# Layer norm of two graph-attention layers: the statistics of a row from an addition with a sum and a Square with a sum

## The chip, the cores and the metric

The kernel runs on one core of a Trainium2 chip. The metric is the device time of one execution in microseconds (us). The kernel before took 1764.37 us, the median of three runs (1763.55, 1764.37 and 1769.72). One further execution was profiled, at 1764.85 us; all views below come from it.

## The reference

Four graph layers on 3327 nodes with 512 features and one adjacency matrix (3327 x 3327 integers, mostly zero). Each layer adds its result to its input and normalises every row:

```
def _layernorm(x, axis=-1, eps=1e-5):
    m = jnp.mean(x, axis=axis, keepdims=True)
    v = jnp.var(x, axis=axis, keepdims=True)
    return (x - m) / jnp.sqrt(v + eps)

x = _layernorm(x + L0(x, adj, W, a1, a2))      # graph attention, 8 heads of 64
x = _layernorm(x + L1(x, adj, ...))            # mean over neighbours
x = _layernorm(x + L2(x, adj, ...))            # mean over the first 64 neighbours
x = _layernorm(x + L3(x, adj, W, a))           # graph attention, 4 heads of 128
```

In layers 0 and 3, for every head, e_ij = leaky_relu(f1_i + f2_j, 0.2) where there is an edge, attention = softmax(e) over j, and the head's result is elu(attention @ Wh), heads side by side. So the row that is normalised is x + elu(h).

## The kernel before

**Tiling.** The nodes lie in 26 blocks of 128 (the partitions). For every block the kernel makes a list of the edges (`structure`, L863) and later gathers one table row per edge with indirect DMAs, issued by GpSimd (POOL): 128 rows at a time are a chunk, up to four chunks a group (`gather`, L1006). A group (`Gat.group`, L1274) compares positions (`far` on ACT, `ds` on DVE), adds scores (`sc` on DVE, L1337 and L1339), takes their Exp on ACT (L1340, L1341), makes the 0/1 selection matrix `sel` (ACT), multiplies the gathered rows by the weights on DVE (L1348, tile `gt`, `gl` or `gk`), and adds them up per node with matmuls on TensorE (PE) into `acc` in PSUM (L1367). Layer 3 has a dense part for the first block's column: `upc` is made on ACT (four instructions, L1404) and DVE (L1406), and goes into `acc` by L1364. Layer 0 has a dense row (`Gat.dense`, L1449: `gd` on ACT, `raw` on DVE, `acct` on PE).

**The end of a block**, in layers 0 and 3 (`Gat.summed`, L1520): ACT divides the heads (`h`, L1518) and takes Exp of them (`e`, L1528); DVE adds max(h, 0) to the residual (`h`, L1530) and then min(e, 1) to that (`e`, L1531). Now `e` is the row to be normalised (the constant -1 of elu does not change a normalised row). `moments` (L803) makes mean and variance with DVE's statistics pass (`st`, L805) and its aggregation (`mv`, L807). The reciprocal root `rs` comes in layer 0 from POOL (`rstd`, two operations, L815 and L816), in layer 3 from Ln and Exp on ACT and three small steps of refinement on DVE (`power`, L831 and L832, and `newton`, L838 to L840). DVE multiplies -mean by `rs` (`nm`, L859) and ACT writes the normalised row (`scaled_by_act`, L860), to `xres` in layer 0 and to `o`, which SP's queue stores to the output, in layer 3. Layer 0 then transposes the row on PE, copies it on ACT (`xt`, L786), multiplies it with one or two weights (`po`, L800), and stores the result for layer 1 (`t`, `zb`).

**What sets the order.** The work is written as generators that yield between stages, and the stages of several blocks and groups are interleaved. Up to L1781 a scheduler then orders each engine's instructions by its own estimates, so layer 0's order can change with any edit. From L1781 on (layers 1 to 3) the order is as written. `rstd` yields `AHEAD` = 2 times ahead of its POOL operations. In layer 0 each tile of a block's end (`h`, `e`, `mv`, `nm`, `rs`) has one buffer, in layer 3 two. Each engine runs its queue in order, and a waiting instruction holds what is behind it.

Of the kernel before, what the change touches and what calls it, by code (L numbers as in the profile page):

```python
# [8 lines left out]
F32 = mybir.dt.float32  # L9
# [8 lines left out]
AF = mybir.ActivationFunctionType  # L18
ALU = mybir.AluOpType
# [4 lines left out]
P = 128  # L24
BIG = 1e30
EPS = 1e-5
# [515 lines left out]
AHEAD = 2  # L542
# [89 lines left out]
def sparse_path(ctx, tc, flag_i, x, adj, l0_w, l0_a1, l0_a2, l1_w_self, l1_b_self, l1_w_nb, l1_b_nb,  # L632
# [13 lines left out]
    nc = tc.nc  # L646
    N, D = x.shape
# [11 lines left out]
    def pool_in(lay, name, bufs=1, **kw):  # L659
        return lay.enter_context(tc.tile_pool(name=name, bufs=bufs, reuse_waits="tile", **kw))  # L660
# [69 lines left out]
    eps = const.tile([P, 1], F32, name="s_eps")  # L730
    nc.gpsimd.memset(eps, EPS)
    mhalf = const.tile([P, 1], F32, name="s_mhalf")
# [22 lines left out]
    H0, _, OUT0 = l0_w.shape  # L755
    H3, _, OUT3 = l3_w.shape
# [12 lines left out]
    def store(dst_d, b, t, shift=0):  # L769
        for p0, p1 in rows_of(b):  # L770
            nc.sync.dma_start(dst_d[shift + b * P + p0:shift + b * P + p1, :], t[p0:p1])
# [7 lines left out]
    def transposed(pool, ps, src, xsum=None, b=0):  # L779

        pt = ps.tile([P, DC, P], F32, name="pt", tag="tr")
        for c in range(DC):
            nc.tensor.transpose(pt[:, c, :], src[:, c * P:(c + 1) * P], ident)  # L783
        xt = pool.tile([P, DC, P], F32, name="xt")
        if xsum is None:
            nc.scalar.copy(xt, pt)  # L786
            return xt
        n = LAST if b == NB - 1 else P
        for c in range(DC):
            nc.scalar.activation(xt[:, c, :n], pt[:, c, :n], AF.Identity, accum_out=xsum[:, c, b:b + 1])  # L790
        if n < P:
            xs = pool.tile([P, DC], F32, name="xs")
            nc.vector.tensor_reduce(xs, xsum, AX.X, ALU.add)
            nc.vector.tensor_scalar(xt[:, :, n], xs, 1.0 / N, None, ALU.mult)
        return xt

    def times(ps, xt, w):
        po = ps.tile([P, D], F32, name="po")
        for c in range(DC):
            nc.tensor.matmul(po, xt[:, c, :], w[:, c], start=c == 0, stop=c == DC - 1)  # L800
        return po

    def moments(fin, y):  # L803
        st = fin.tile([P, 6], F32, name="st")
        nc.vector.bn_stats(st, y)  # L805
        mv = fin.tile([P, 2], F32, name="mv")
        nc.vector.bn_aggr(mv, st)  # L807
        return mv

    def rstd(fin, mv):  # L810

        for _ in range(AHEAD):
            yield
        rs = fin.tile([P, 1], F32, name="rs")
        nc.gpsimd.tensor_scalar(rs, mv[:, 1:2], EPS, 1.0, ALU.add, ALU.mult)  # L815
        nc.gpsimd.tensor_tensor(rs, rs, mhalf, ALU.pow)  # L816
        yield
        return rs

    def root(fin, mv):  # L820

        r0 = fin.tile([P, 1], F32, name="r0")
        nc.scalar.activation(r0, mv[:, 1:2], AF.Sqrt, bias=eps)
        yield
        nc.vector.reciprocal(r0, r0)
        return newton(fin, mv, r0)
# [27 lines left out]
    def scaled(o, y, mv, rs):  # L854
        nc.vector.tensor_scalar(o, y, mv[:, 0:1], rs, ALU.subtract, ALU.mult)  # L855

    def scaled_by_act(o, y, fin, mv, rs):
        nm = fin.tile([P, 1], F32, name="nm")
        nc.vector.scalar_tensor_tensor(nm, mv[:, 0:1], -1.0, rs, ALU.mult, ALU.mult)  # L859
        nc.scalar.activation(o, y, AF.Identity, bias=nm, scale=rs)  # L860


    def structure(big, mid, ps, m0):  # L863
# [167 lines left out]
    class Gat:  # L1031
# [488 lines left out]
        def summed(self, fin, acc, xb):  # L1520

            hq = acc
            if isinstance(acc, list):
                hq = fin.tile([P, D], F32, name="h")
                self.divided(fin, acc, hq)
                self.held[acc.turn] = 0
            e = fin.tile([P, D], F32, name="e")
            nc.scalar.activation(e, hq, AF.Exp)  # L1528
            yield
            nc.vector.scalar_tensor_tensor(hq, hq, 0.0, xb, ALU.max, ALU.add)  # L1530
            nc.vector.scalar_tensor_tensor(e, e, 1.0, hq, ALU.min, ALU.add)  # L1531
            mv = moments(fin, e)
            rs = yield from (rstd if self.k == 0 else power)(fin, mv)
            return e, mv, rs

    def by_heads(w, c, H):

# [18 lines left out]
    xres = [wpool.tile([P, D], F32, name=f"xres{b}") for b in range(NB)]  # L1556
# [17 lines left out]
    with ExitStack() as pro:  # L1574
# [18 lines left out]
        g0 = Gat("g0", t0_d, H0, OUT0, w0, 0)  # L1593
# [91 lines left out]
    fin = pool_in(lay, "l0f", side="right")  # L1685
# [4 lines left out]
    def layer0(b, acc):  # L1690
        work.add(layer0_end(b, acc))

    def layer0_end(b, acc):
        yield
        x1 = xres[b]
        e, mv, rs = yield from g0.summed(fin, acc, x1)
        scaled_by_act(x1, e, fin, mv, rs)
        xt = transposed(fin, ps, x1)
        yield
        t2 = fin.tile([P, 2, D], F32R, name="t2", bufs=2)  # L1700
        po = times(ps, xt, wn)
        nc.scalar.copy(t2[:, 0], po)
        nc.vector.tensor_sub(t2[:, 1], po, t2[:, 0].bitcast(F32))
        store(t1_d, b, t2.bitcast(F32).rearrange("p s d -> p (s d)"), 2)
        if b >= NB - LATE0:
            return
        if b:
            yield
        zb = fin.tile([P, D], F32, name="zb0", tag="e")
        nc.scalar.copy(zb, times(ps, xt, wx))  # L1710
        store(z1_d, b, zb)
# [140 lines left out]
    def both():  # L1852
        work.step()
        ends.step()
# [9 lines left out]
    with ExitStack() as lay:  # L1864
        fin = pool_in(lay, "l1f", 2)
# [91 lines left out]
        for item in woven(ring):  # L1957
            b, at = item[0], item[4]
# [33 lines left out]
    with ExitStack() as lay:  # L1992
        fin = pool_in(lay, "l2f", 2)
# [6 lines left out]
        g3 = Gat("g3", t3_d, H3, OUT3, w3, 1)  # L2000
# [84 lines left out]
    with ExitStack() as lay:  # L2085
        pools = (Ring(H3 * (OUT3 + 2), extra, rows), pool_in(lay, "l3s", 3),
                 pool_in(lay, "l3pa", 2, space=PSUM), pool_in(lay, "l3p1", 3, space=PSUM))
        fin = pool_in(lay, "l3f", 2)

        def layer3(b, acc):  # L2090
            ends.add(layer3_end(b, acc))

        def layer3_end(b, acc):
            yield
            e, mv, rs = yield from g3.summed(fin, acc, xres[b])
            o = fin.tile([P, D], F32, name="o")
            scaled_by_act(o, e, fin, mv, rs)
            store(out, b, o)

        def verdict():  # L2100

            yield
            bad = fin.tile([P, 4, NL], F32, name="bad")
            nc.vector.memset(bad, 0.0)
            nc.vector.tensor_tensor(bad[:, 0, :], deg[:, 1:], cnt, ALU.not_equal)
            used = fin.tile([P, 3, NL], F32, name="used")
            room = fin.tile([P, 3, NL], F32, name="room")
            nc.vector.tensor_add(used[:, 1:], starts.rearrange("p l s -> p s l"), dgs.rearrange("p l s -> p s l"))
            nc.vector.tensor_add(used[:, 0], used[:, 1], used[:, 2])
            for ls in lists:  # L2110
                for l in ls:
                    for k, n in enumerate((l.room, l.near, l.far)):
                        nc.gpsimd.memset(room[:, k, l.at:l.at + 1], float(n))
            yield
            nc.vector.tensor_tensor(bad[:, 1:], used, room, ALU.is_gt)
            tot = fin.tile([P, 2], F32, name="tot")
            nc.vector.tensor_reduce(tot[:, 0:1], bad, AX.XY, ALU.add)
            nc.vector.tensor_reduce(tot[:, 1:2], spread, AX.X, ALU.add)
            nc.vector.tensor_add(tot[:, 0:1], tot[:, 0:1], tot[:, 1:2])
            yield  # L2120
            pt = pools[3].tile([P, 512], F32, name="pg")
            nc.tensor.matmul(pt[0:1, 0:1], tot[:, 0:1], ones[:, 0:1], start=True, stop=True)
            nc.vector.tensor_copy(flag_i, pt[0:1, 0:1])

        ends.newest = True
        ends.add(g3.open_column(fin))
        for k, item in enumerate(groups(pools[0], range(1, NB), first=(1, 2))):
            if item[4] == 0:
                ends.add(g3.column(item[0], fin))
            work.add(g3.group(item, pools, accs, layer3, sall))  # L2130
            both()
            if k == 6:
                ends.add(layer3_end(0, bias1))
            if k == 12:
                ends.add(verdict())
        while work.live or ends.live:
            both()


@with_exitstack  # L2140
def kernel(ctx: ExitStack, tc: tile.TileContext, *args):


    nc = tc.nc
    pool = ctx.enter_context(tc.tile_pool(name="flagp", bufs=1))
    flag_i = pool.tile([1, 1], I32, name="flag_i")
    sparse_path(tc, flag_i, *args)
    again = nc.values_load(flag_i[0:1, 0:1], min_val=0, max_val=1 << 20)
    with tc.If(again > 0):
        general_path(tc, *args)  # L2150
# [30 lines left out]
```

## Time and profile before

| what | us |
|---|---|
| runs shown, median (range) | 1764.37 (1763.55 to 1769.72) |
| profiled execution | 1764.85 |
| its span, first to last instruction | 1763.1 |
| layer 0: lists and projection, then groups with ends | 0 to 290, 290 to 735 |
| layers 1 and 2 | 735 to 1475 |
| layer 3 | 1475 to 1763 |
| L805 (`st`), 104 in all four layers, 26 in each | 0.695 each (median) |
| L807 (`mv`), 104 | 0.182 each (median) |
| L1531 (`e`), 52 in layers 0 and 3 | 0.692 each (median) |

In the profile, busy time is given for each engine: PE for matmuls, PEld for weight loads, DVE for VectorE, ACT for ScalarE, POOL for GpSimd. The chain of work that ended last is followed back from the last instruction to what released each step; an engine's share in it is time for which this engine was what everything waited for. A timeline row gives start, duration, engine, line, operation, output and input tiles, and in square brackets how long the engine had been idle and what ended that. A stretch is a window of the span with the busy time of each engine in it, the granted TensorE clock, the busy share of the DMA engines and GB/s. A source row gives the smallest, median and largest duration in ns.

### The profile page before, as it was taken

What the parts mean: (1) busy time and instruction counts of PE and PEld (TensorE: products, weight loads), DVE (VectorE), ACT (ScalarE), POOL (GpSimd) and SP (SyncE); (2) the same over time, 40 slices, a digit from 0 to 9 for tenths busy, and PEclk for the clock granted to TensorE, in tenths of its full rate; (3) what the DMA queues carried; (4) which work ended last, traced back from release to release, by engine and by line L of the source; (5) the groups of instructions that cost most, each with busy time, mean ns of one, the idle gap of its engine ahead of it and who ended that gap; (6) DMA issues with size and microseconds to landing.
All of it is one profiled execution on the core that took longest, in us unless ns stands there. A gap on an engine that the chain in (4) does not pass through costs nothing.

```text
span 1763.1 us, 24351 instructions
## 1 busy us (share of the span) xinstructions
PE 1505.3 (85%) x7266; PEld 1002.5 (57%) x7266; DVE 1219.4 (69%) x3292; ACT 872.8 (50%) x2922; POOL 760.5 (43%) x909
## 2 busy tenths in 40 slices
PE   5979847889999989889999999856999973878885
PEld 4756536656666667445555554422666752767664
DVE  8989859988668788225656785537666542867897
ACT  5879645656657767312122121211444442556786
POOL 3000146555454620164444652266656206666640
PEclk9989878999999999889999999988999996979998
DMA  8787667666665542298988995387878416767761
GB/s 258 260 274 240 210 190 247 216 185 200 189 188 154 173 123 80 82 401 292 303 287 306 342 371 191 98 285 247 279 255 269 153 43 189 198 199 211 225 198 56
DMA packets 130401, 381.98 MB, mean 217 GB/s; under 512 B 22037, under 2 KB 36477, under 8 KB 130259
## 3 DMA queue, kind: packets, MB, share of 16 engines
q0 software_dynamic: 67696, 252.97, 45.2%
q1 hardware_dynamic: 62563, 127.35, 21.4%
q8 instruction: 60, 0.98, 0.2%
q14 instruction: 82, 0.67, 0.1%
HBM read 331.89 MB, written 48.37 MB: 216 GB/s over the span
## 4 chain that ended last, share of the span: by engine, by line
PE 57%; DVE 17%; ACT 9%; issue 7%; another core or an unknown queue 4%; DMA 3%; POOL 2%; SPq 0%; DVEq 0%; POOLq 0%; ACTq 0%
PE po L800 18%; PE acc L1367 10%; PE acc L1844 9%; PE po L1048 8%; PE pt L783 3%; DVE cand L912 2%; DVE gt L1348 2%; DVE gl L1348 1%; PE acc L1836 1%; DVE st L805 1%; PE acct L1477 1%; PE acc L1255 1%; ACT h L1518 1%; DVE e L1531 1%
## 5 line engine op out<-in xcount | busy, mean ns | idle before, releaser
L1010 POOL DMA_INDIRECT gt<-t_d,idx x201 | 204.0, 1015 | 369.0 <-DVE mx L1147 197.4
L1010 POOL DMA_INDIRECT gl<-t_d,idx x265 | 261.6, 987 | 185.7 <-issue 56.7
L1367 PE MATMUL acc<-gt,sel 128*128 128x264 f32 (+3 forms) x804 | 208.2, 404 | 3.4 <-issue 1.9
L800 PE MATMUL po<-wn,xt 128*128 128x512 f32 x416 | 197.5, 618 | 15.5 <-ACT xt L786 5.8
L1010 POOL DMA_INDIRECT gm<-t_d,idx x138 | 136.1, 986 | 132.7 <-PE acc L1844 79.1
L1367 PEld LDWEIGHTS acc<-gt,sel 128*128 128x128 f32 (+3 forms) x804 | 150.7, 197 | 41.0 <-issue 15.9
L1367 PE MATMUL acc<-gl,sel 128*128 128x260 f32 (+3 forms) x524 | 140.3, 412 | 14.5 <-issue 11.0
L800 PEld LDWEIGHTS po<-wn,xt 128*128 128x128 f32 x416 | 79.3, 197 | 101.8 <-issue 79.4
L1048 PE MATMUL po<-gt,xt 128*128 128x268 f32 x416 | 115.9, 424 | 15.2 <-ACT xt L790 10.9
L1348 DVE TENSOR_TENSOR gt<-gt,pg 128x1536 f32<-128x1536 f32 (+3 forms) x63 | 116.4, 1848 | 14.8 <-ACT sel L1343 12.5
L1367 PEld LDWEIGHTS acc<-gl,sel 128*128 128x128 f32 (+3 forms) x524 | 100.6, 202 | 34.7 <-issue 15.6
L1844 PE MATMUL acc<-gm,selr 128*128 128x512 f32 (+3 forms) x324 | 106.6, 452 | 5.5 <-DMA gm<-t_d,idx 5.1
L1010 POOL DMA_INDIRECT gk<-t_d,idx x65 | 67.4, 1037 | 95.5 <-DMA t_d<-mean 58.6
L912 DVE MAX8 cand<-val 128x8 f32<-128x464 uint16 (+32 forms) x184 | 107.8, 622 | 0.0
L1048 PE MATMUL po<-w,xt 128*128 128x262 f32 x416 | 98.7, 391 | 9.6 <-ACT xt L790 5.8
L786 ACT COPY xt<-pt 128x512 f32<-128x512 f32 x81 | 46.9, 587 | 119.3 <-PE pt L783 83.6
L1048 PEld LDWEIGHTS po<-gt,xt 128*128 128x128 f32 x416 | 78.6, 202 | 34.7 <-ACT xt L790 14.5
L1300 ACT ACTIVATE far<-place,nmids 128x384 int16<-128x384 int16 (+3 forms) x167 | 88.2, 544 | 13.8 <-DVE ds L1310 9.9
L1048 PEld LDWEIGHTS po<-w,xt 128*128 128x128 f32 x416 | 78.9, 192 | 27.3 <-ACT xt L790 10.0
L800 PE MATMUL po<-wx,xt 128*128 128x512 f32 x208 | 93.5, 594 | 0.0
L800 PE MATMUL po<-wl,xt 128*128 128x512 f32 x208 | 93.0, 592 | 0.0
L783 PE MATMUL pt<-s_ident,xres 128*128 128x128 f32 x500 | 78.8, 285 | 10.4 <-DVE xres L855 5.3
(377 smaller groups left out, 3268.5 us busy)
## 6 DMA issues: line engine op xcount, KB each, us to landing
ab<-in_adj_dram SPq DMA_DIRECT2D x25, 832.0 KB
ab<-in_adj_dram SPq DMA_DIRECT2D x25, 831.5 KB
t_d<-t SPq DMA_DIRECT2D x25, 512.0 KB
gm<-t_d POOLq DMA_DIRECT2D x23, 512.0 KB
t_d<-t SPq DMA_DIRECT2D x25, 384.0 KB
t_d<-tg SPq DMA_DIRECT2D x25, 264.0 KB
gd<-t_d SPq DMA_DIRECT2D x25, 264.0 KB
t_d<-tg SPq DMA_DIRECT2D x25, 260.0 KB
```

What stands on the lines that cost most here:

```text
L783: nc.tensor.transpose(pt[:, c, :], src[:, c * P:(c + 1) * P], ident)
L786: nc.scalar.copy(xt, pt)
L800: nc.tensor.matmul(po, xt[:, c, :], w[:, c], start=c == 0, stop=c == DC - 1)
L805: nc.vector.bn_stats(st, y)
L912: nc.vector.max(out=cand[:, s, :], in_=val[:, cuts[s]:cuts[s + 1]])
L1010: nc.gpsimd.indirect_dma_start(out=t[:m, c, :], out_offset=None, in_=table[:, :], in_offset=bass.IndirectOffsetOnAxis(ap=l.idx[:m, c0 + c: ...
L1048: nc.tensor.matmul(pw[s], xt[:, c, :], self.w[:, c, s, :], start=c == 0, stop=c == DC - 1)
L1255: nc.tensor.matmul(self.acc[h // hh][:, h % hh, :], wt[:m, h, :], G[:m, h, :], start=False, stop=False)
L1300: nc.scalar.activation(o, place[:, (c0 + q0) * P:(c0 + q1) * P], AF.Abs, bias=l.nmid[:, k:k + 1], scale=2.0)
L1348: nc.vector.tensor_mul(Gc[:, :, :OUT], Gc[:, :, :OUT], w[:, :g].rearrange("p c (h o) -> p (c h) o", o=1).to_broadcast([P, g * H, OUT]))
L1367: nc.tensor.matmul(accs[b][s], S[:m, c, :], G[:m, c, s * hh * M:(s + 1) * hh * M], start=at + c == 0, stop=last)
L1844: nc.tensor.matmul(accs[b], chosen, parts[:, k * D:(k + 1) * D], start=at + c + k == 0, stop=k == top and at + c == n - 1)
```

## The change

The row's sum comes out of the addition L1531 (`accum_out`, a sum along the row); DVE turns it into -mean with one multiplication of a 128x1 column. ACT squares the centred row (`e` plus -mean as a bias column) with a sum of its own, which gives 512 times the variance; the squares themselves go into `h`, which is not needed any more. `moments` is not called in these two layers. `rs` is made from the second sum with the same operations as before (POOL in layer 0; Ln, Exp and three steps on DVE in layer 3), the factor 1/512 taken into their constants. The last product is -mean times `rs`. Layers 1 and 2 are as before.

```diff
-    def rstd(fin, mv):
...
-    def scaled_by_act(o, y, fin, mv, rs):
-        nm = fin.tile([P, 1], F32, name="nm")
-        nc.vector.scalar_tensor_tensor(nm, mv[:, 0:1], -1.0, rs, ALU.mult, ALU.mult)
-        nc.scalar.activation(o, y, AF.Identity, bias=nm, scale=rs)
+    def scaled_by_act(o, y, nm, rs):
+        nc.vector.tensor_mul(nm[:, 0:1], nm[:, 0:1], rs)
+        nc.scalar.activation(o, y, AF.Identity, bias=nm[:, 0:1], scale=rs)
...
             nc.vector.scalar_tensor_tensor(hq, hq, 0.0, xb, ALU.max, ALU.add)
-            nc.vector.scalar_tensor_tensor(e, e, 1.0, hq, ALU.min, ALU.add)
-            mv = moments(fin, e)
-            rs = yield from (rstd if self.k == 0 else power)(fin, mv)
-            return e, mv, rs
+            nm = fin.tile([P, 2], F32, name="nm")
+            nc.vector.scalar_tensor_tensor(e, e, 1.0, hq, ALU.min, ALU.add, accum_out=nm[:, 0:1])
+            nc.vector.tensor_scalar(nm[:, 0:1], nm[:, 0:1], -1.0 / D, None, ALU.mult)
+            nc.scalar.activation(hq, e, AF.Square, bias=nm[:, 0:1], accum_out=nm[:, 1:2])
+            if self.k == 0:
+                for _ in range(AHEAD):
+                    yield
+                rs = fin.tile([P, 1], F32, name="rs")
+                nc.gpsimd.tensor_scalar(rs, nm[:, 1:2], 1.0 / D, EPS, ALU.mult, ALU.add)
+                nc.gpsimd.tensor_tensor(rs, rs, mhalf, ALU.pow)
+                yield
+            else:
+                r0 = fin.tile([P, 1], F32, name="r0")
+                nc.scalar.activation(r0, nm[:, 1:2], AF.Ln, bias=eps, scale=1.0 / D)
+                nc.scalar.activation(r0, r0, AF.Exp, scale=-0.5)
+                yield
+                rs = fin.tile([P, 1], F32, name="rs")
+                nc.vector.scalar_tensor_tensor(rs, nm[:, 1:2], EPS * D, r0, ALU.add, ALU.mult)
+                nc.vector.scalar_tensor_tensor(rs, rs, -0.5 / D, r0, ALU.mult, ALU.mult)
+                nc.vector.scalar_tensor_tensor(rs, rs, 1.5, r0, ALU.add, ALU.mult)
+            return e, nm, rs
```

The two callers, `layer0_end` (L1693) and `layer3_end` (L2093), hand `nm` on in place of `mv`.

More of the change, by code (lines that the diff above doesn't have):

```diff
@@ L808, in moments @@
         return mv
-    def rstd(fin, mv):
[L812 to L818, printed above, removed]
     def root(fin, mv):
@@ L1695, in layer0_end @@
         x1 = xres[b]
-        e, mv, rs = yield from g0.summed(fin, acc, x1)
-        scaled_by_act(x1, e, fin, mv, rs)
+        e, nm, rs = yield from g0.summed(fin, acc, x1)
+        scaled_by_act(x1, e, nm, rs)
         xt = transposed(fin, ps, x1)
@@ L2094, in layer3_end @@
             yield
-            e, mv, rs = yield from g3.summed(fin, acc, xres[b])
+            e, nm, rs = yield from g3.summed(fin, acc, xres[b])
             o = fin.tile([P, D], F32, name="o")
-            scaled_by_act(o, e, fin, mv, rs)
+            scaled_by_act(o, e, nm, rs)
             store(out, b, o)
```

## The prediction

> **What bounds the kernel now.** I read the page's busy row and the chain's shares first, then the busy time by stretch, then the timeline of DVE and ACT around the ends of blocks, and last the waits.
>
> ```profile
> PE 1505.3 (85%) x7266; PEld 1002.5 (57%) x7266; DVE 1219.4 (69%) x3292; ACT 872.8 (50%) x2922; POOL 760.5 (43%) x909
> ...
> PE 57%; DVE 17%; ACT 9%; issue 7%; another core or an unknown queue 4%; DMA 3%; POOL 2%; SPq 0%; DVEq 0%; POOLq 0%; ACTq 0%
> ```
>
> Over the whole span PE carries the chain; DVE has 17% of it. The change touches only the ends of blocks in layer 0 (290 to 735 us) and layer 3 (1500 to 1763 us), so the stretches count (us, then busy time of PE, PEld, DVE, ACT, POOL):
>
> ```profile
> 290.00:400.00 110.00, 93.53 (x462) 65.62 (x463) 96.23 (x303) 67.21 (x198) 61.62 (x63) 0.89 0.67 209
> 400.00:500.00 100.00, 94.92 (x438) 63.31 (x437) 71.75 (x204) 62.54 (x200) 50.22 (x61) 1.00 0.63 190
> 600.00:735.00 135.00, 121.02 (x673) 88.32 (x672) 98.57 (x194) 87.82 (x331) 24.09 (x28) 0.96 0.32 99
> 1600.00:1700.00 100.00, 83.18 (x527) 66.62 (x528) 85.74 (x225) 76.28 (x236) 63.01 (x65) 0.95 0.75 219
> ```
>
> Layer 0 is DVE's until 400 (96 of 110), PE's to 600, then shared. In layer 3 from 1600 on DVE and ACT are both nearly full. There the timeline shows a loop. DVE, one block:
>
> ```profile
> 1689.76 0.69 DVE L1530 SCALAR_TENSOR_TENSOR h<-h,xres 128x512 f32<-128x512 f32 x1
> 1690.49 0.69 DVE L1531 SCALAR_TENSOR_TENSOR e<-e,h 128x512 f32<-128x512 f32 x1
> 1691.21 0.69 DVE L805 BATCH_NORM_STATS2 st<-e 128x6 f32<-128x512 f32 x1
> 1691.94 0.18 DVE L807 BATCH_NORM_AGGREGATE mv<-st 128x2 f32<-128x6 f32 x1
> 1692.04 1.19 DVE L1348 TENSOR_TENSOR gl<-gl,pg 128x1024 f32<-128x1024 f32 x1
> ```
>
> and ACT in the same block:
>
> ```profile
> 1689.10 0.63 ACT L1528 ACTIVATE e<-h 128x512 f32<-128x512 f32 x1
> ...
> 1690.84 0.60 ACT L1300 ACTIVATE far<-place,nmids 128x384 int16<-128x384 int16 x1
> 1692.16 0.29 ACT L831 ACTIVATE r<-mv,s_eps 128x1 f32<-128x1 f32 x1 [0.72 <-DVE mv L807]
> ...
> 1696.83 0.63 ACT L1528 ACTIVATE e<-h 128x512 f32<-128x512 f32 x1
> ```
>
> DVE's addition starts 0.03 after the Exp ends (1689.73); four DVE instructions later Ln starts (1692.16) after an idle 0.72; from Ln ACT runs without a gap to the next Exp's end (1697.46), where DVE's next addition starts. The period, 7.73, is 2.43 of DVE and 5.30 of ACT, and DVE is full meanwhile too.
>
> **The change, part by part** (us per block; 26 blocks in each layer).
>
> DVE loses st and mv. In the loop above the product L1348 starts 1.55 after e's start. Afterwards e's addition carries an accumulator read, and one 128x1 multiply follows. Nearest rows:
>
> ```profile
> L926 DVE TENSOR_SCALAR_CACHE_REDUCE some<-sl x25: 160/177/203, 44.1 to 415.2; 128x24 f32<-128x24 f32 x17, 128x32 f32<-128x32 f32 x5, 128x40 f32<-128x40 f32 x2, 128x48 f32<-128x48 f32 x1
> L926 DVE DVE_READ_ACCUMULATOR some<-sl x25: 77/84/90, 44.2 to 415.3; 128x1 f32 x25
> ...
> L790 ACT ACTIVATION_READ_ACCUMULATOR xt<-pt x208: 194/222/323, 17.6 to 1444.9; 128x1 f32 x104
> ```
>
> The read starts some 0.07 before its addition ends and takes 0.08, so the sum stands about 0.70 after e's start. The multiply starts 0.03 later (the gap between L838 and L839) and takes 0.15 (L928); an independent product may start 0.10 after it (mv to L1348 above). That is 0.84 in place of 1.55: **DVE gains 0.71 per block**, if the addition stays at 0.69 with a sum. No row here has a large addition with a sum. From below it is 0.69; from above 1.22: 0.69 holds 512 elements and about 0.16 of fixed cost (the 128x1 rows), so half the rate adds 0.53. I take 0.69, since L926 at 24 to 48 elements is only 0.03 above the 128x1 rows, and keep 1.22 for the range.
>
> [...]
>
> ACT gains a Square of 128x512 with a column as bias. Exp without a column is 0.63 and L860 with two is 0.80 (layer 3): 0.72 between them; then the read, 0.20 (L884: 0.18 to 0.20), starting 0.10 before the Square ends. In ACT's queue that is 0.62 + 0.09 = **0.71 per block**; from below 0.53 (Exp's slot), from above 0.94. Ln and Exp stay, and both programs load three tables.
>
> The path from e to Ln: sum 0.70, multiply to 0.885, 0.04 to cross (mv to Ln), Square and read 0.82, 0.035 to Ln: 1.78 after e's start, in place of 1.67 (1690.49 to 1692.16): **0.12 later**. ACT's idle 0.72 covers the Square: it is free at 1691.44, the multiply is done at about 1691.38. Where that cover is gone, the 0.71 is paid whole. The product nm x rs takes the place of L859 at the same 0.16; layer 0's two POOL operations stay two. The junk output goes into h, which the same engine rewrites later, in order: no new wait for a buffer.
>
> Queued behind the new wait (Square for the multiply) are ACT's upc x4, Exp of the scores, sel and far; DVE waits for upc, PE for sel.
>
> **Layer 3.** For each block I took from the timeline how late DVE starts h after the Exp. Blocks 0 to 7 (to 1620): PE and the gathers decide; L1340 waits 1.3 to 12.1 in seven of the eight, which hides 0.12: nothing. From block 8 on:
> - DVE late by 0.38 to 0.86 (into blocks 9, 12, 13, 20, 21), or ACT itself waiting 1.46 for DVE's sc (into 14): DVE's 0.71 counts until ACT's path, 0.12 later, decides: into 9, 12, 13, 14, 20, 21 that is -0.70, -0.71, -0.30, -0.71, -0.32, -0.60 = -3.34.
> - Exp on time, late by 0.03 or held by upc (into 10, 16 to 19, 25, and the tail after 25): 7 x 0.12 = +0.84.
> - the other five (into 11, 15, 22, 23, 24), with smaller slack either way: +0.10, -0.03, 0, -0.10, 0 = -0.03.
> Sum -2.5.
>
> **Layer 0.** Ends at 302, 333 and 354 lie on the chain while it runs on DVE: 3 x -0.71 = -2.1. From 400 to 600 PE is at 94 of 100 and hides both. From 640 to 690 the chain alternates between DVE (st, raw) and ACT (gd, h): three ends, 0.71 off the one and on the other, 0, bounds 2.1 either way. Four ends from 684 to 723 are serial from e through POOL to ACT (2.8 to 3.9 each): 4 x 0.12 = +0.5. SP's queue swaps two stores with loads, POOL's gathers pass some rs; PE's order differs in 34 places. I price these at 0. Sum -1.6.
>
> Together -4.1 on the profiled execution's 1764.85 (span 1763.1 and 1.75 around it): 1760.75. That execution lies 0.5 above the median, 1764.37, less than all else here. **Forecast 1761**, within 0.5% (8.8 us), which is about what a measurement of this kernel can tell from no change.
>
> **Rivals.**
>
> 1, slower: the addition with its sum takes 1.22. Then DVE gains only 0.18 and Ln is 0.65 late. Layer 3: 7 x 0.65, the late periods -0.1 each, the other five +0.5 each: +6. Layer 0: DVE's gain shrinks to -0.5 and the round trip through POOL grows by 0.65 in the 14 ends at which
>
> ```profile
> DVE nm L859 <- POOL rs L816: 16.9, 16, 2.9
> ACT xres L860 <- DVE nm L859: 17.1, 14, 3.6
> ```
>
> (us in total, times, longest) show DVE and ACT already waiting; half behind PE: +4.6. Together +10: 1775. It decides from an addition of about 0.84 on, where the -4.1 is used up (14 us for 0.53). [...]
>
> 2, slower: ACT becomes layer 0's bound. 26 Squares are 18.5 of ACT in front of copies that PE waits for (vc, xt, h: 13.8 of PE's waits there). Half of it through: +9.2 - 2.1 - 2.5 = +4.6, 1769.5; all of it: +13.9, 1779. Against it: ACT is busy 65% there and PE has other groups to run.
>
> 3, faster: DVE's gain comes through wherever DVE is full in layer 0 (290 to 425 and 600 to 705, 12 ends x 0.71 = -8.5), and ACT's idle time covers 0.12 in layer 3 (-3.3): 1753.
>
> 4, the change doesn't do what it says in layer 0: the new order there outweighs the operations. The longest single wait of a block's end is 5.8 (h for its Exp): 6 either way, 1755 to 1767.
>
> **How the numbers follow.** Forecast 0.46 (0.38 within, 0.08 faster), rival 1 0.12 (0.10 slower, 0.02 within), rival 2 0.19 (0.14 slower, 0.05 within), rival 3 0.18 (0.17 faster, 0.01 within), rival 4 0.05 (0.02 faster, 0.02 within, 0.01 slower). Faster 0.27, within 0.48, slower 0.25. The forecast's own range is 1756 to 1768 (Square 0.53 to 0.94, layer 0's 2.1 either way). The range for 8 in 10 reaches into rivals 1 to 3: 1750 to 1777.
>
> **What would show it.** Right: e at 0.69 with a read of 0.08; Square near 0.72; DVE's busy time about 52 x 0.64 = 33 lower (0.695 + 0.18 - 0.08 - 0.15), ACT's some 48 higher; Ln about 1.8 after e's start; periods from 1690 to 1713 still 7.7 to 8.1; DVE no longer full from 1671 to 1741. Wrong: e near 1.2 (rival 1); PE below 90 of 100 between 400 and 600 with waits on ACT (rival 2); layer 0 shorter by over 5 (rival 3).

## The result, and the profile after

The changed kernel takes 1763.06 us (median of 22 runs, 1752.86 to 1779.07), the kernel before, run beside it, 1767.71 (22 runs, 1758.43 to 1776.47): a ratio of 0.9973, 95% interval 0.9954 to 0.9991, so 4.65 us less, where 4.1 less were forecast. In a second measurement the ratio was 0.9939 [0.9917, 0.9961] (the experiment after_again; the plain medians there, 1771.26 and 1777.51, give 0.9965). The profiled execution of the first measurement has a span of 1769.0 us, some 8 above what the median leaves for it, so its stretches tell where work lies, and not to the microsecond how long a stage is.

The page of the changed kernel, busy row and chain's shares:

```profile
PE 1514.6 (86%) x7266; PEld 1006.2 (57%) x7266; DVE 1187.4 (67%) x3292; ACT 911.9 (52%) x3026; POOL 753.8 (43%) x909
...
PE 59%; DVE 14%; ACT 9%; issue 8%; DMA 4%; another core or an unknown queue 3%; POOL 2%; SPq 0%; ACTq 0%; POOLq 0%; DVEq 0%
```

DVE is busy 32.0 us less, ACT 39.1 more, and DVE's share of the chain falls from 17% to 14%. The new operations, by source row of the changed kernel (smallest, median, largest ns):

```profile
L1521 DVE SCALAR_TENSOR_TENSOR e<-e,h x51: 676/691/694, 305.9 to 1759.1; 128x512 f32<-128x512 f32 x51
L1521 DVE DVE_READ_ACCUMULATOR e<-e,h x51: 76/81/84, 306.5 to 1759.8; 128x1 f32 x51
```

```profile
L1523 ACT ACTIVATE h<-e,nm x51: 705/722/724, 306.8 to 1760.1; 128x512 f32<-128x512 f32 x51
L1523 ACT ACTIVATION_READ_ACCUMULATOR h<-e,nm x51: 185/187/192, 307.5 to 1760.7; 128x1 f32 x51
...
its engine sat idle before it (us, times) until:
  DVE nm L1522: 20.4, 19
```

The addition with a sum takes the 0.69 that it took without one. (The rows count 51 of 52: in layer 3's first block the tile has another name.) The stretches of the changed kernel that answer to those of before (PE, PEld, DVE, ACT, POOL, clock, DMA share, GB/s):

```profile
290.00:400.00 110.00, 95.45 (x496) 67.41 (x495) 99.91 (x323) 73.54 (x215) 64.62 (x66) 0.93 0.70 217
400.00:500.00 100.00, 93.52 (x422) 61.11 (x421) 64.53 (x193) 66.60 (x207) 48.10 (x57) 0.98 0.61 186
600.00:735.00 135.00, 122.29 (x672) 88.64 (x673) 95.96 (x196) 94.50 (x357) 25.31 (x30) 0.95 0.33 99
1600.00:1700.00 100.00, 86.40 (x536) 68.55 (x535) 81.79 (x234) 86.00 (x261) 65.96 (x66) 0.91 0.76 217
```

In layer 3, from 1600 on, DVE and ACT have changed places: before, DVE 86 and ACT 76 of 100; now 82 and 86. The loop that the prediction read, in the same block (the 17th end of layer 3) of the changed kernel, DVE first:

```profile
1695.71 0.69 DVE L1519 SCALAR_TENSOR_TENSOR h<-h,xres 128x512 f32<-128x512 f32 x1 [0.18 <-issue]
1696.44 0.69 DVE L1521 SCALAR_TENSOR_TENSOR e<-e,h 128x512 f32<-128x512 f32 x1
1697.06 0.08 DVE L1521 DVE_READ_ACCUMULATOR e<-e,h 128x1 f32 x1
1697.17 0.15 DVE L1522 TENSOR_SCALAR nm<-nm 128x1 f32<-128x1 f32 x1
1697.24 1.21 DVE L1337 TENSOR_TENSOR gl<-gl,pg 128x1024 f32<-128x1024 f32 x1
```

and ACT:

```profile
1695.05 0.63 ACT L1517 ACTIVATE e<-h 128x512 f32<-128x512 f32 x1
...
1696.79 0.60 ACT L1289 ACTIVATE far<-place,nmids 128x384 int16<-128x384 int16 x1
1697.36 0.72 ACT L1523 ACTIVATE h<-e,nm 128x512 f32<-128x512 f32 x1
1697.99 0.19 ACT L1523 ACTIVATION_READ_ACCUMULATOR h<-e,nm 128x1 f32 x1
1698.21 0.29 ACT L1533 ACTIVATE r<-nm,s_eps 128x1 f32<-128x1 f32 x1
...
1702.89 0.63 ACT L1517 ACTIVATE e<-h 128x512 f32<-128x512 f32 x1
```

The product starts 0.80 after e (1.55 before), Ln 1.77 after e (1.67 before). From Ln to the end of the next Exp ACT still takes 5.31 without a gap, so the period is 2.53 + 5.31 = 7.84, 0.11 more than 7.73, although DVE now has idle time in it (0.18 ahead of h).

### The profile page after: what moved, and what is told of

The parts are those of the page before. It is cut to its first block, busy times and chain, and to the rows that moved or that the text cites. A ratio compares the mean times of both kernels' runs of the same rounds, so it can differ in the third digit from the quotient of the medians.

```text
span 1769.0 us, 24447 instructions
## 1 busy us (share of the span) xinstructions
PE 1514.6 (86%) x7266; PEld 1006.2 (57%) x7266; DVE 1187.4 (67%) x3292; ACT 911.9 (52%) x3026; POOL 753.8 (43%) x909
## 4 chain that ended last, share of the span: by engine, by line
PE 59%; DVE 14%; ACT 9%; issue 8%; DMA 4%; another core or an unknown queue 3%; POOL 2%; SPq 0%; ACTq 0%; POOLq 0%; DVEq 0%
PE po L800 18%; PE acc L1356 12%; PE acc L1850 9%; PE po L1037 9%; PE pt L783 3%; DVE cand L901 2%; DVE gt L1337 2%; PE acc L1244 1%; PE acc L1842 1%; DMA gm<-t_d,idx 1%; ACT h L1507 1%; DVE val L888 1%; ACT gd L1457 1%; PE acc L1929 1%
## 5 line engine op out<-in xcount | busy, mean ns | idle before, releaser
L786 ACT COPY xt<-pt 128x512 f32<-128x512 f32 x81 | 47.0, 588 | 119.5 <-PE pt L783 93.7
```

## The experiments

**Theory** at the start: what counts is that DVE is rid of 0.71 a block, in layer 3 wherever DVE is late for the Exp, in layer 0 wherever DVE is on the chain. **Rivals**: the addition's sum or the Square costs what DVE gains; layer 0's new order, not its operations, makes the difference.

Two yardsticks are used below, both from the profiles: layer 0 by the time of its 26 additions e after the first of them, and the last part of layer 3 from the addition h of its ninth end to the start of the last scaling. Each group of four kernels shares one chip and its runs of the kernel before (median 1675.12 us for the first four, 1777.51 for the next, 1675.74 for the last), and the three chips are different ones.

### Each layer alone

l3_only has the old end in layer 0 (`self.k == 0`, with `rstd` and the old scaling back), l0_only the same with `self.k == 1`, the old end in layer 3:

```diff
             nc.vector.scalar_tensor_tensor(hq, hq, 0.0, xb, ALU.max, ALU.add)
+            if self.k == 0:
+                nc.vector.scalar_tensor_tensor(e, e, 1.0, hq, ALU.min, ALU.add)
+                mv = moments(fin, e)
+                rs = yield from (rstd if self.k == 0 else power)(fin, mv)
+                return e, mv, rs
```

> Only layer 3 has the new end; layer 0 keeps the statistics pass and POOL's root of its variance. The recorded account: layer 3 from block 8's h to the last scaling took 136.7 us before and 134.9 in the changed kernel; here it should be 134.9 within 0.5, the part of layer 0 (first e to last scaling) as before, 420.7 within 4, and the total 2 to 3 us under the kernel before (ratio about 0.9985). Rival, the new order in layer 0 makes the gain: the total is as before (ratio 1.000), and layer 0 alone shows the 4.6 us. Rival, ACT as the bound: layer 3 over 137.

> Only layer 0 has the new end; layer 3 keeps the statistics pass. The recorded account: layer 3's stretch from block 8 as before, 136.7 within 0.5; layer 0 about 1.6 us shorter, total ratio about 0.999. Rival, order in layer 0: total about 4 us shorter (ratio 0.9975), with no single operation to put it down to. Rival, ACT in front of PE's copies in layer 0: total 4 to 9 us longer (ratio 1.002 to 1.005), and PE's waits on ACT between 290 and 735 grow beyond the 25 us or so of before.

Measured: l3_only 0.9975 [0.9958, 0.9991], 1671.57 us; l0_only 0.9968 [0.9954, 0.9982], 1669.87 us; l0_only a second time on another chip (l0_again below) 0.9957 [0.9943, 0.9972]. Both halves gain. The last part of layer 3 takes 131.40 us with the new end and 133.75 with the old, 2.35 less (forecast 2.5). This yardstick is steady at the faster pace: the three profiles with the new end in layer 3 (l3_only, new_ahead1, new_ahead3) give 131.30 to 131.40, the three with the old end (l0_only, l0_again, l0_keep) 133.71 to 133.81. Layer 0 takes 4.9 less (412.7 against 407.8 in the table below), where 1.6 were forecast; the ratio of l0_only, 0.9968, is nearer to the 0.9975 of the rival that puts the gain down to the order.

The traces also settle what the halves are made of: in layer 0, PE, DVE, ACT and POOL run the same instructions in the same order in l3_only as in the kernel before, and in l0_only as in the changed kernel.

### The pass put back, in both layers

keep_stats is the changed kernel with the statistics pass and its aggregation on DVE behind the multiply; nobody uses their result.

```diff
+            moments(fin, e)
             nc.scalar.activation(hq, e, AF.Square, bias=nm[:, 0:1], accum_out=nm[:, 1:2])
```

> The changed kernel with DVE's statistics and aggregation kept as dead work behind the multiplication in layers 0 and 3 (their result is not used). It takes away DVE's gain of 0.71 us per block and keeps ACT's Square and the 0.12 on the path to Ln. The recorded account: layer 3 from block 8's h to the last scaling 137.5 to 139 us (the changed kernel 134.9, before 136.7), because the late blocks lose their 0.7 and the others stay at +0.1; the total 1 to 4 us over the kernel before (ratio 1.0005 to 1.002). Rival, the gain is not DVE's but the order's: the total stays 4 us under before. Rival, the addition with a sum matters: it is 0.69 again, so this one expects nothing new.

Measured: 1.0012 [0.9996, 1.0028], 1676.68 us: the gain is gone. The timeline of DVE in layer 3 of keep_stats:

```profile
1632.25 0.69 DVE L1521 SCALAR_TENSOR_TENSOR e<-e,h 128x512 f32<-128x512 f32 x1
1632.86 0.08 DVE L1521 DVE_READ_ACCUMULATOR e<-e,h 128x1 f32 x1
1632.98 0.15 DVE L1522 TENSOR_SCALAR nm<-nm 128x1 f32<-128x1 f32 x1
1633.05 0.68 DVE L805 BATCH_NORM_STATS2 st<-e 128x6 f32<-128x512 f32 x1
1633.77 0.18 DVE L807 BATCH_NORM_AGGREGATE mv<-st 128x2 f32<-128x6 f32 x1
1633.87 1.19 DVE L1337 TENSOR_TENSOR gl<-gl,pg 128x1024 f32<-128x1024 f32 x1
```

The path from e to the Square is that of the changed kernel; only the product starts late again, 1.62 after e. The last part of layer 3 takes 135.51 us: 4.1 more than without the pass (131.40), and 1.8 more than the old end (133.75). In layer 3 the order is as written, and in this part DVE's two added instructions a block are all that differs from l3_only in what the engines run. So there the pass that DVE is rid of is worth 4.1, and the rest of the new end (Square, multiply, the later Ln) costs 1.8.

### A second Square

two_squares issues one more Square, without a sum, ahead of the real one.

```diff
+            nc.scalar.activation(hq, e, AF.Square, bias=nm[:, 0:1])
             nc.scalar.activation(hq, e, AF.Square, bias=nm[:, 0:1], accum_out=nm[:, 1:2])
```

> The changed kernel with the Square done twice on ACT in layers 0 and 3 (the first one without a sum, its result overwritten). Each costs a slot of 0.62 us in ACT's queue. The recorded account: in layer 3 nearly every block from 10 on now waits for ACT, so about 13 of 18 periods grow by 0.62: block 8's h to the last scaling about 143 us (134.9 with one); in layer 0 PE covers most: 0 to 3 us; the total 5 to 9 us over the changed kernel with one Square, so 0 to 5 us over the kernel before (ratio 1.000 to 1.003). Rival, ACT has room in layer 3: under 137 there. Rival, ACT is what bounds layer 0: layer 0 alone grows by 8 us or more, the total ratio is over 1.005.

Measured: 1.0086 [1.0064, 1.0108], 1687.44 us. The timeline of ACT in layer 3 of two_squares:

```profile
1628.91 0.71 ACT L1523 ACTIVATE h<-e,nm 128x512 f32<-128x512 f32 x1
1629.65 0.72 ACT L1524 ACTIVATE h<-e,nm 128x512 f32<-128x512 f32 x1
1630.28 0.19 ACT L1524 ACTIVATION_READ_ACCUMULATOR h<-e,nm 128x1 f32 x1
1630.49 0.30 ACT L1534 ACTIVATE r<-nm,s_eps 128x1 f32<-128x1 f32 x1
```

Ln is 0.74 later, and mostly nothing hides it: the periods of 7.8 to 8.05 become 8.6 to 8.8, 14 of the 17 steps from the tenth end to the last scaling grow by 0.68 to 0.98, and the last part of layer 3 takes 142.31, 10.9 more than in l3_only. So after the change ACT's path decides most periods there. In the block read above, the first Square was cheap because ACT waited at that place anyway (0.72 in the kernel before). The expectation had layer 3 nearly right (143), but not the total, 1.000 to 1.003: layer 0, from the first e to the last scaling, takes 416.0, 5.3 more than in l0_only, where 0 to 3 were expected. Its rival for layer 0 had 8 or more. Layer 0's order is again another one here, so the 5.3 are not ACT's alone by this run.

### Is the changed kernel the sum of its halves? The order of layer 0

after_again is the changed kernel on the chip of old_ahead1, old_ahead3 and late_dve. old_ahead1 and old_ahead3 are the kernel before, new_ahead1 and new_ahead3 the changed kernel, with another constant: the same instructions, issued in another order around the ends of layer 0.

```diff
-AHEAD = 2
+AHEAD = 1
```

> The changed kernel as it is, beside the kernel before and the three kernels below, on one chip. Its two halves alone gave -0.25% (layer 3) and -0.32% (layer 0). Theory 1, the halves add up, since layers 0 and 3 are separated by 740 us of layers 1 and 2: ratio 0.9943, some 9 to 10 us, with layer 0 (first e to last scaling) some 5 below the old one and layer 3 from block 8 on some 2.3 below. Theory 2, the changed kernel's order in layer 0 (which no half has to the letter) loses part of layer 0's gain again: ratio near 0.9973 as in the first measurement, layer 3 from block 8 on still 1.8 to 2.4 shorter, layer 0 within 1.5 of the old one.

> The kernel before with AHEAD = 1 in place of 2: the same instructions, in another order around the ends of layer 0's blocks. Theory (the order of layer 0 is worth some microseconds either way, whatever the operations): layer 0, from first e to last scaling, differs by 2 to 5 us from the kernel before, and the time with it; layer 3 and layers 1 and 2 as before. Rival (the operations alone set the time, the order is worth under 1 us): ratio 0.9995 to 1.0005, layer 0 within 1 us.

> The kernel before with AHEAD = 3 in place of 2: the same instructions, a third order. Theory (order is worth microseconds): layer 0 differs by 2 to 5 us from the kernel before, not in the direction that AHEAD = 1 takes by rule, so that the two and the kernel before spread over 3 us or more. Rival (operations alone): within 1 us of the kernel before.

> The changed kernel with AHEAD = 1 in place of 2, to stand beside the kernel before with AHEAD = 1 (1.0083 of the kernel before). Theory 1 (the new ends are worth some 0.4 to 0.6% in any order, since the work that DVE is rid of is the same): 1.0025 to 1.0045. Theory 2 (what the new ends gain in layer 0 is an accident of the order that came with them): layer 3 alone keeps its 0.15 to 0.25%, and layer 0 may go either way by 5 us and more: 1.0035 to 1.0095 or under 1.0000.

> The changed kernel with AHEAD = 3, to stand beside the kernel before with AHEAD = 3 (0.9971). Theory 1 (new ends worth 0.4 to 0.6% in any order): 0.991 to 0.993, the best so far. Theory 2 (an accident of the order): layer 3's 0.15 to 0.25% alone is sure, 0.995 to 0.998 or anything else by layer 0's order.

| AHEAD | old end, ratio to the kernel before | new end |
|---|---|---|
| 1 | 1.0083 [1.0054, 1.0111] | 0.9958 [0.9942, 0.9974] |
| 2 | 1 | 0.9973 [0.9954, 0.9991] and 0.9939 [0.9917, 0.9961] |
| 3 | 0.9971 [0.9948, 0.9993] | 0.9973 [0.9960, 0.9986] |

The halves (0.25% and 0.32 to 0.43%) make 0.57 to 0.68% together; the second measurement has 0.61% (0.35% by its plain medians), the first 0.27%. With these intervals, a sum of the halves and a loss of part of it cannot be told apart. What after_again's theory 2 says of the order is out, though: as shown above, the changed kernel has in layer 0 the order of l0_only. Theory 1 of the runs with AHEAD, that the new end is worth the same in any order, fell: with AHEAD = 3 the new end is worth nothing measurable (0.9973 against 0.9971), with AHEAD = 1 some 1.2% (old and new end were measured on different chips, each against its own runs of the kernel before). The order of the same instructions, 0.9971 to 1.0083 with the old end, is worth more than this change. Layer 0 as one stretch, in the kernel before (302 to 723, first measurement) and in old_ahead1 (304 to 742, another chip):

```profile
302.00:723.00 421.00, 383.87 (x1949) 269.13 (x1949) 331.93 (x841) 274.46 (x929) 184.66 (x203) 0.97 0.53 161
```

```profile
304.00:742.00 438.00, 389.90 (x1951) 270.37 (x1949) 331.77 (x840) 276.94 (x929) 181.65 (x203) 0.96 0.51 155
```

DVE's work is the same to 0.2 us and PE's 6 longer; the stretch is 17 us longer (the median of all runs is 17 us above the kernel before too, the ratio makes it 15), so most of it is waiting. The new end came out at 0.994 to 0.997 in all three orders. In new_ahead3 layer 0, from the first e to the last scaling, is 4.6 us shorter than in l3_only (410.9 against 415.5), and the way from there to layer 3's first scaling 4.4 longer (748.8 against 744.4), so in these two profiles the gain is given back behind layer 0.

### The pass put back in layer 0 alone

l0_again is l0_only once more, l0_keep the same with the unused pass.

```diff
             nc.vector.tensor_scalar(nm[:, 0:1], nm[:, 0:1], -1.0 / D, None, ALU.mult)
+            if self.k == 0:
+                moments(fin, e)
             nc.scalar.activation(hq, e, AF.Square, bias=nm[:, 0:1], accum_out=nm[:, 1:2])
```

> The new end in layer 0 only, once more, beside the next kernel. Before: 0.9968 [0.9954, 0.9982]. Expected again 0.996 to 0.998.

> The new end in layer 0 only, with DVE's statistics pass and aggregation kept behind the multiply, their result unused: DVE is as busy as before, the row's sums come as in the changed kernel. Theory (DVE's relief is layer 0's gain, where DVE is full): the gain goes, 0.999 to 1.001. Rival 1 (the new order is the gain): 0.996 to 0.998 as without the pass. Rival 2 (both, as the first five ends, 3.5 us shorter with or without the pass, suggest): halfway, 0.998 to 0.999. Each kernel's order differs a little, so a result outside all three speaks for the order.

Measured: 0.9957 [0.9943, 0.9972] without the pass, 0.9989 [0.9977, 1.0001] with it. So with the pass back 4.8 us are lost, the theory's answer. It is not a clean test, though: the scheduler gave l0_keep another order in layer 0 than l0_only has, on PE at 41 places (39 between the kernel before and the changed kernel, counted in the same way). keep_stats has exactly l0_keep's order there, on the chip of l0_only and l3_only. Where the time is lost says more (start of the n-th addition e after the first one, us):

| kernel | 2nd | 4th | 6th | 15th | 18th | 22nd | 26th | 6th to 26th |
|---|---|---|---|---|---|---|---|---|
| l3_only (old end) | 28.4 | 77.5 | 119.5 | 240.1 | 279.0 | 356.8 | 412.7 | 293.2 |
| l0_only | 26.2 | 73.9 | 115.9 | 239.1 | 276.4 | 353.5 | 407.8 | 291.9 |
| l0_again | 26.2 | 74.0 | 115.2 | 238.9 | 276.1 | 353.7 | 408.0 | 292.8 |
| l0_keep | 29.2 | 75.9 | 115.8 | 240.0 | 278.3 | 357.1 | 413.2 | 297.3 |
| keep_stats | 29.4 | 76.9 | 115.9 | 239.9 | 278.4 | 357.5 | 413.6 | 297.7 |

l0_only and l0_again are the same program on two chips and agree within 0.9, l0_keep and keep_stats, with the same layer 0, within 1.0, so differences of 2 us can be read. By the sixth end the four kernels with the new end lead by 3.6 to 4.3, with the pass or without. At the second and fourth end the pass seems to cost 2 to 3, but up to there PE's order in l0_keep is nearly the old end's. That the lead is the same with the pass speaks against DVE's relief as its cause. An order alone can do as much: old_ahead3 reaches its sixth end after 116.4 and the kernel before after 122.9 (both at the slower pace). Which moved instruction does it here was not tried, so the cause of the lead stays open.

From the sixth end on, the old end takes 293.2, the new one 291.9 to 292.8, the new one with the pass 297.3 to 297.7. On the one chip of l3_only, l0_only and keep_stats that is 5.8 more with the pass than without, and 4.5 more than the old end. Read as operations, the pass is worth 4.5 to 5.8 there, and the rest of the new end costs 4.1 to 4.5, nearly all of it. But the order differs between these kernels as well, and an order alone moved the same stretch from 294.9 (before) to 298.5 (old_ahead3) and 317.4 (old_ahead1). So this split is argued, not shown. In two_squares, again in an order of its own, one more pass on ACT goes with about as much: 162.5 and 137.5 us from the sixth to the 18th end and on to the last scaling, against 160.5 and 134.3 in l0_only. The stretch from 560 to 700, in l3_only, l0_only and l0_keep:

```profile
560.00:700.00 140.00, 127.28 (x722) 94.78 (x720) 107.88 (x212) 95.58 (x366) 32.91 (x36) 0.95 0.34 106
```

```profile
560.00:700.00 140.00, 129.20 (x724) 95.76 (x722) 102.57 (x211) 101.44 (x383) 29.28 (x35) 0.95 0.33 104
```

```profile
560.00:700.00 140.00, 126.32 (x719) 94.46 (x718) 109.05 (x231) 102.89 (x388) 30.48 (x35) 0.95 0.33 102
```

PE is at 126 to 129 of 140, ACT 6 busier with the new end, DVE 6 busier with the pass than without. No engine is full, and yet kernels with 0.7 us more a block on either of two engines are slower there. That the ends are chains in which both take part is how the prediction read its chain; no run shows it.

### A later Square, and the last scaling on DVE

late_dve tries to give ACT back what the Square took, in layer 3: the Square goes behind the next Exp, the last scaling to DVE.

```diff
+            if self.k:
+                yield
             nc.scalar.activation(hq, e, AF.Square, bias=nm[:, 0:1], accum_out=nm[:, 1:2])
...
-            scaled_by_act(o, e, nm, rs)
+            nc.vector.tensor_mul(nm[:, 0:1], nm[:, 0:1], rs)
+            nc.vector.tensor_scalar(o, e, rs, nm[:, 0:1], ALU.mult, ALU.add)
```

> The changed kernel with layer 3's Square issued one stage later, behind the next block's Exp, so that it finds its multiply long done, and layer 3's last scaling on DVE in place of ACT (0.71 of ACT's queue less, some 0.47 of DVE more per block). Theory (after the change ACT's queue, from Ln to the next Exp, sets layer 3's periods of 7.84 to 8.05 while DVE has some 0.9 idle in each): these periods fall to 7.3 to 7.5, eight of them, so that layer 3 from block 8 on is 3 to 4 us shorter than in the changed kernel, and the time is 0.2% below it. Rival 1 (DVE is the limit again as soon as it has the scaling): periods 7.7 to 8.1, no gain or up to 2 us slower. Rival 2 (gathers or TensorE set these periods): periods within 0.1 of the changed kernel's.

Measured: 0.9957 [0.9932, 0.9982], beside 0.9939 [0.9917, 0.9961] for the changed kernel on the same chip: no gain. The last part of layer 3 takes 139.46 in its profile, 139.65 in the changed kernel's. DVE in one period of late_dve:

```profile
1692.85 0.69 DVE L1519 SCALAR_TENSOR_TENSOR h<-h,xres 128x512 f32<-128x512 f32 x1
...
1695.14 0.55 DVE L2106 TENSOR_SCALAR o<-e,rs,nm 128x512 f32<-128x512 f32 x1
...
1700.62 0.69 DVE L1519 SCALAR_TENSOR_TENSOR h<-h,xres 128x512 f32<-128x512 f32 x1 [0.17 <-issue]
```

and what waited for whom there, from 1690 on (total us, times, longest):

```profile
ACT pg L1329 <- DVE sc L1328: 7.5, 6, 1.9
PEld acc L1353 <- DVE upc L1395: 7.4, 6, 2.9
```

In this period, 7.77, DVE is idle for 0.17, and ACT waits for DVE: rival 1, DVE is the limit as soon as it has the scaling. The expected 7.3 to 7.5 left out that DVE's own work is then 7.6. The next two periods are longer, 9.14 and 9.09; in each DVE waits 1.5 for PE's `acc`, so they are neither engine's alone. The profiled execution, at 1780.70, is also the slowest of this kernel's 12 runs (median 1774.72). Of all kernels tried, none beats the changed one beyond its interval.

## Why the prediction was right, and where its steps were not

The forecast, 4.1 us less and within 0.5%, fits the first measurement, 4.65 [1.6 to 8.1]. By the stages it is a right sum for layer 3 and too small a one for layer 0, and that the total came out so near is partly luck: the two halves, measured alone, add up to 0.57% or more, over 9 us.

- **Operations: right.** e 0.691 with a read of 0.081 (0.69 and 0.08); Square 0.722 (0.72); product 0.80 after e (0.84); Ln 1.77 after e (1.78); DVE 32.0 less (33). ACT 39.1 more, not 48: 48 took Square and read as 0.92 each, but the read starts 0.09 before the Square ends, so that 52 of them are 42, and 3 of these overlap with ACT's instructions beside them. The prediction's own slot of 0.71 would have given 37.
- **Rival 1 is out.** The addition kept its 0.69: both sources are f32, and 512 elements with a sum took 0.691, without one 0.692 (medians). The 1.22 of the range and of this rival put the 512 elements at half the rate; that was the author's estimate, and no run shows an addition at that rate.
- **Layer 3: right, -2.35 (chip of l3_only) and -1.76 (first measurement) for -2.5.** In the first measurement, from profile to profile, the late periods gave what was forecast: -0.64 into block 9, -0.64 into 12, -0.71 into 14, -0.30 into 20 (-0.70, -0.71, -0.71, -0.32). Where ACT's path decided, it was +0.11, +0.11, +0.10 into 16, 17, 18 and +0.11 in the tail (+0.12 each). Wrong were above all into 10 (-0.69 for +0.12), into 11 (+1.29 for +0.10), into 21 (-0.25 for -0.60) and into 13 (-0.08 for -0.30); together they are 0.95 above the forecast, more than the 0.7 by which the sum is off. Smaller misses, such as into 25 (-0.10 for +0.12), go both ways. Into 11 is not the change's: in l3_only that period is 0.75 shorter than in l0_only. The exchange was right in kind: the pass gone is worth 4.1, the rest of the new end costs 1.8.
- **Layer 0: the step that failed.** The forecast took 3 ends x -0.71 ahead of 400, nothing from 400 to 690 and +0.5 behind: -1.6. Measured at the faster pace: -3.6 to -4.3 by the sixth end, then -0.4 to -1.3. The first number is not the mechanism that the step named, since the lead is the same with the pass put back. The new order, which the forecast priced at 0, can make as much; that it does so here was not tried. After the sixth end the result is near what was forecast (-0.4 to -1.3 against some +0.5), but the runs read as two large terms that nearly cancel: 4.5 to 5.8 for DVE's pass and 4.1 to 4.5 for the rest of the new end, with the order mixed into both. "PE hides both" held for the stretch from the sixth to the 18th end only roughly (+1.0 to +1.4 for the new end, 1.6 to 2 more with the pass). In the first measurement the two profiles show no gain in layer 0 at all (420.7 before, 421.1 after), but they cannot resolve it (last section).
- **The other rivals.** Rival 2 was half right, as far as the split above holds: ACT's Square and what comes with it cost some 4 in layer 0 and not 9 to 14, and the rest of the change pays for it. Rival 3 had -8.5 for DVE's relief in layer 0; with the pass put back 4.8 were lost. Rival 4 was set too small: 6 either way, where the order alone moved the total by 15 to 17 in old_ahead1.

## What to carry to other kernels

Moving a pass from one engine to another is worth the difference of two prices, and each has to be measured by itself: put the removed pass back unused, and double the added one. In layer 3's loop, where two engines hand work to each other, relief of 0.7 on DVE made ACT the limit at a period 0.11 longer, and handing the scaling to DVE made DVE the limit again in the period read. Where a scheduler orders a stage, change the order alone (one constant) before an effect of a few microseconds is put down to the operations, and compare the order in the traces: a pass put back can change it too.

## What the runs showed that was not expected

- Two paces: the kernel before took 1767.71 us in the first measurement and 1777.51 on the chip of after_again, but 1675.12 and 1675.74 on two other chips. The difference lies mostly outside the yardsticks used here: from layer 0's last scaling to layer 3's first 792.7 in the kernel before, 744.4 in l3_only; up to the first e 302.3 against 283.5; the first eight ends of layer 3 112.5 against 93.5. What makes it was not tried. In l3_only's chain from 1518 to 1600 the gathers still have 23%.
- The same layer 0, first e to last scaling, takes 410.7 and 410.8 on the two faster chips (l0_only, l0_again), and 421.1 and 416.0 (the changed kernel) at the slower pace, where the profiled executions fell 8 us above and 9 below their medians: there, one profile does not resolve 5 us.
- DVE's read of the sum takes 0.081 and starts 0.07 before the addition ends; ACT's takes 0.187 and starts 0.09 before the Square ends. From the Square's start to the next operation that uses its sum it is 0.85.
